# A second Strassen level for one product of each projection, residual sums by accumulating transfers, and longer staging rings, in a four-layer graph-attention kernel

## The chip, the cores and the metric

The kernel runs on one core of a Trainium2 chip. A core has a matrix engine (TensorE, PE in the profile; its weight loads are shown apart as PEld), three engines for elementwise work (VectorE or DVE, ScalarE or ACT, GpSimd or POOL), a queue engine (SyncE or SP) that issues transfers, and 16 DMA engines. Matrix products read on-chip memory (SBUF) and write a small accumulator memory (PSUM, eight banks of 128 x 512 float32); in this kernel DVE and ACT read PSUM, POOL works on SBUF alone. The metric is the device time of one execution in microseconds; less is better.

## What is computed

Input `x` holds 128 graphs of 64 nodes with 512 features, all float32. Four layers follow, each `x = x + f(relu(layernorm(x)))`, and all four see the same 64 x 64 adjacency mask:

```python
# layer 0: 8 heads of 64; q, k, v with bias
x = x + softmax(q @ k.T / 8 + mask) @ v
# layer 1: the same with an output projection
x = x + (softmax(q @ k.T / 8 + mask) @ v) @ Wo + bo
# layer 2: no softmax; one head
rel = adj.T * (q @ k.T);  rel = rel / norm(rel, axis=2)
x = x + rel @ v
# layer 3: attention as in layer 1, then o = o @ Wp + bp
x = x + o + layernorm(o) * gamma + beta
```

## The kernel before

**Tiling.** The 8192 rows are cut into 16 blocks of 512 rows a layer, 64 blocks in all, numbered `n`; `l = n // 16` is the layer. For each block the kernel computes `hT`, the normalised block turned so that features lie on partitions, by a layer norm (DVE statistics, ACT scaling) and transposing transfers (`turn`: a DVE copy that splits each float32 in two 16-bit planes `z`, a DMA transpose into `hp`, an ACT copy back). The four tiles `z` and three tiles `hp` are the "plane rings".

**Projections.** Each weight product of a block is 512 x 512 x 512. `projection` does it by Strassen's method in Winograd's form: seven products of 256 x 256 x 256 in place of eight. The operands are quarters of `hT` and four sums of them in `S` (`sums_x`, on POOL; for the output projection, quarters of `oT` and `SO`), and quarters of the weight and sums of them (`sums_w`). One product is four matmul calls of 128 x 128 stationary by 256 moving columns (`prod_T`, `prod_N`), and each float32 call is two records in the trace. The products run in `ORDER = (1, 6, 5, 2, 7, 3, 4)`; the results are combined by ACT (`s1`, `z5`, `Y11`), DVE (`u2`, `u3`, `Y12`, `Y21`) and POOL (`Y22`). Product 4 is the right lower quarter of the block times the weight sum `WT4`; its result gives the quarter `Y21` with one sum. There are 3, 4, 2 and 4 projections a block in layers 0 to 3. In layer 2, q and k are folded into one matrix beforehand.

**Attention.** `attend` issues the 64 x 64 score products of a block into `so` tiles (two PSUM banks each, two of them), masks them (DVE), subtracts the maximum (POOL), exponentiates (ACT), normalises (POOL), turns the weights by transposing transfers, and issues the products with `v`. `relate` is its counterpart in layer 2. The `mm` tiles (four banks) serve the projections.

**Residuals.** `load_xo` reads the block of `x` again into `xo` and adds a row (bias or beta) to it with four POOL additions. In layer 1 the output projection's `emit_out1` adds straight into `xo`. In layer 3 the projection goes to a tile `o` in the buffer `kT`; `tail3` takes its statistics, adds `o` to `xo` with four POOL additions, then two DVE operations a quarter (`z<-kT,mv,row` and `xo<-z,rs,xo`) finish the block.

**Order.** The program records all operations first (`Plan.record`). `Plan.order` then sorts them: it simulates five queues with a duration for every operation (`duration`), takes on each queue the ready step with the lowest rank, and the order that results is what is issued. On the chip each engine works through its own list in order and waits on semaphores, so a list that was built on a wrong duration makes an engine wait. All recorded operations are issued at line 193. Generators (`spawn`, with delays in "ticks" of one product) decide when a step is recorded.

Of the kernel before, what the change touches and what calls it, by code (L numbers as in the profile page):

```python
# [18 lines left out]
P = 128  # L19
# [24 lines left out]
ORDER = (1, 6, 5, 2, 7, 3, 4)  # L44
ORDER0 = (1, 2, 5, 6, 3, 7, 4)
# [10 lines left out]
class Plan:  # L56
# [4 lines left out]
    def __init__(self, nc):  # L61
        self.nc = nc
        self.steps, self.products = [], []
        self.wrote, self.readers, self.known = {}, {}, {}
        self.group = None
        for e in ("tensor", "vector", "scalar", "gpsimd", "sync"):
            setattr(self, e, Engine(self, e))
# [48 lines left out]
    def add(self, eng, calls, reads, writes, busy, late):  # L116
# [12 lines left out]
        self.steps.append((eng, calls, deps, busy, late))  # L129

    def order(self):
        n = len(self.steps)
        wait = [len(s[2]) for s in self.steps]
        users = [[] for _ in range(n)]
        for i, s in enumerate(self.steps):
            for d in s[2]:
                users[d].append(i)

        rank = [i - RUSH * any(v.tensor.name.startswith("mm_") for c in s[1] for v in c[1][1:] if isinstance(v, bass.AP)) for i, s in enumerate(self.steps)]
# [10 lines left out]
        while len(out) < n:  # L150
# [17 lines left out]
            eng, _, _, busy, late = self.steps[i]  # L168
            if e == "sync":
                moved = max(moved, at + 1400) + late / 180  # L170
                late = moved + 600 - at - busy
            elif e == "vector" and late == PORT:
                busy += max(0.0, free["gpsimd"] - at)
                port = at + busy
            elif e == "gpsimd":
                busy += max(0.0, port - at)
            free[e] = at + busy
            out.append((at, i))
            for u in users[i]:
                same = self.steps[u][0] == e  # L180
                ready[u] = max(ready[u], at + busy + (0.0 if same and e != "sync" else late))
# [36 lines left out]

PORT = 150.5
RUSH = 60  # L220
# [4 lines left out]
def duration(eng, op, aps, a, k):  # L225
# [3 lines left out]
    if eng == "tensor":  # L229
# [3 lines left out]
        pass_ = max(n, P if m > HD else HD) * 0.842  # L233
# [17 lines left out]
    if eng == "gpsimd":  # L251
        if n <= HD:
            return (1010 if ALU.pow in a else 310), 120
        return n * (1.82 if n > D else 2.41), 120
    size = (2 if out.dtype == U16 else 4) * n * out.partition_size()
    return 1270 if k.get("transpose") else 520, size
# [3 lines left out]
def gnn_stack_kernel(  # L260
# [17 lines left out]
    def pool(name, bufs, **kw):  # L278
        return Ring(ctx.enter_context(tc.tile_pool(name=name, bufs=1, **kw)), bufs)

    const, wp, p1, p2, p4, p8, p3 = (
        pool("const", 1), pool("w", 4), pool("p1", 1), pool("p2", 2), pool("p4", 4), pool("p8", 8), pool("p3", 3),
    )
    rows = pool("rows", 3)
    sm = pool("sm", 4)
    dram = ctx.enter_context(tc.tile_pool(name="dram", bufs=1, space=bass.MemoryType.DRAM))
    ps_mm = pool("ps_mm", 4, space=bass.MemoryType.PSUM)
    ps_so = pool("ps_so", 2, space=bass.MemoryType.PSUM)
# [10 lines left out]
    pw = ps_mm.tile([P, KC, P], F32, tag="mm", name="pw")  # L299
# [3 lines left out]
    def dma(dst, src):  # L303
        plan.sync.dma_start(dst, src)

# [36 lines left out]
    def load_w(name, src):  # L342

        w = wp.tile([P, 7, 2, H2], F32, tag="w", name=name)


        def part(i, j):
            return src[i * H2 : (i + 1) * H2, j * H2 : (j + 1) * H2].rearrange("(c p) f -> p c f", p=P)

        dma(w[:, W11], part(0, 0))  # L350
        dma(w[:, W21], part(1, 0))
        dma(w[:, WT3], part(0, 1))
        dma(w[:, W22], part(1, 1))
        return w

    def sums_w(w, eng):
        tt = eng.tensor_tensor
        tt(w[:, WT1], w[:, WT3], w[:, W11], ALU.subtract)
        tt(w[:, WT2], w[:, W22], w[:, WT1], ALU.subtract)
        yield 1  # L360
# [3 lines left out]
    W = {}  # L364

    def weight(name, src, eng=gps):
        W[name] = load_w(name, src)
        yield 4
        yield from sums_w(W[name], eng)

# [4 lines left out]
    first = [load_w("q0", wq0)]  # L375
# [4 lines left out]
    first += [load_w("k0", wk0)]  # L380
# [16 lines left out]
    def raw(tag, src, nm):  # L397
        t = p1.tile([P, KC, D], F32, tag=tag, name=nm)
        for c in range(KC):
            dma(t[:, c, :], src[c * P : (c + 1) * P, :])  # L400
            yield 3
        return t

    def fold():
# [4 lines left out]
        for dc in range(KC):  # L409
            pa = ps_mm.tile([P, D], F32, tag="mm", name=f"pfa_{dc}")  # L410
# [4 lines left out]
            f = p4.tile([P, D], F32, tag="z", name=f"fa_{dc}")  # L415
            act.copy(f, pa)
            yield 1
# [4 lines left out]
        for ec in range(KC):  # L422
            f = p4.tile([P, KC, P], F32, tag="z", name=f"ft_{ec}")
            turn(f, rv[:, ec, :], f"v2_{ec}")
            yield 1
            dma(v2d.rearrange("(c p) e -> p c e", p=P)[:, :, ts(ec, P)], f)
            yield 1
# [17 lines left out]
    hTs, Ss, vs = {}, {}, {}  # L445
    ready = set()

    def turn(dst, src, nm):


        zp = p4.tile([P, D], F32, tag="z", name=f"zp_{nm}").bitcast(U16).rearrange("p (w f) -> p w f", w=2)
        dve.tensor_copy(zp, src.bitcast(U16).rearrange("p (f w) -> p w f", w=2))
        hp = p3.tile([P, 2, KC, P], U16, tag="hp", name=f"hp_{nm}")
# [5 lines left out]
    def layer_norm(n):  # L459
# [19 lines left out]
        if n == 0:  # L479
            for t in range(NT):  # L480
                z = xins[n][t]
                act.activation(z, z, AF.Relu, bias=nb[:, t : t + 1], scale=rs[:, t : t + 1])
                pt = ps_mm.tile([P, KC, P], F32, tag="mm", name=f"pz_{n}_{t}")
# [4 lines left out]
                if t == 1:  # L488
                    for i in range(WARM // 2):
                        pe.transpose(pw[:, i % KC, :], xins[n][0][:, ts(i % KC, P)], ident)  # L490
                (dve.tensor_copy if t else act.copy)(hT[:, :, ts(t, P)], pt)
        for t in range(NT) if n else ():
# [8 lines left out]
    def sums_x(tag, src, nm, eng):  # L501
# [7 lines left out]
        return {1: x11, 2: x12, 3: S[:, 3], 4: x22, 5: S[:, 0], 6: S[:, 1], 7: S[:, 2]}  # L509
# [19 lines left out]

    def projection(prod, w, xop, nm, emit, order=ORDER):  # L530

# [3 lines left out]
        def bank(i):  # L535
            banks[i] = ps_mm.tile([P, D], F32, tag="mm", name=f"pp{i}_{nm}")
# [6 lines left out]
        X = {1: 1, 2: 1, 6: 6, 7: 6, 5: 5, 3: 5, 4: 4}  # L543
        for i in order:
# [4 lines left out]
            prod(ps, w[:, BLOCKS[i]], xop()[i], first)  # L549
# [16 lines left out]
            elif i == 3:  # L566
                emit("Y12", ps, tmp["u2"])
            if i != order[-1]:
# [4 lines left out]
    def emit_plain(region):  # L573

        def emit(what, a, b=None):
# [15 lines left out]
    def emit_bias(region, bias):  # L591

        def emit(what, a, b=None):
# [37 lines left out]
    def scores(qT, kT, g, nm):  # L631

        pss = ps_so.tile([P, 2, 2, KC, G], F32, tag="so", name=f"pss_{nm}")
        for p in range(2):
            for c in range(KC):
                for h, x in QUARTERS:
                    b = h ^ x
                    at = ts(4 * g + 2 * p + b, G)  # L640
                    pe.matmul(
                        pss[half(x), b, p, c, :], qT[half(h), c, at], kT[half(h), c, at], start=True, stop=True
                    )
        return pss

    def attend(n, qT, kT, v, done):

        l = n // NB
        plan.begin()
        psss = [scores(qT, kT, g, f"{n}_{g}") for g in range(2)]  # L650
        plan.end(300)
        ss = [p4.tile([P, 2 * KC, 2, G], F32, tag="s", name=f"s_{n}_{g}") for g in range(2)]
        yield 1
        for s, pss in zip(ss, psss):
            for b in range(2):
                dve.tensor_tensor(
                    s[:, :, b, :], pss[:, b].rearrange("p q c j -> p (q c) j"),
                    MASKS[l].unsqueeze(1).to_broadcast([P, 2 * KC, G]), ALU.add,
                )
            sf = s.rearrange("p q b j -> p (q b) j")  # L660
# [3 lines left out]
            yield 2  # L664
        yield 1
        for s in ss:
# [6 lines left out]
            yield 2  # L673
        yield 1

        aTs = []
        for s in ss:
            aT = s.rearrange("p (q c) b j -> p q c (b j)", q=2)
            aTs.append(aT)
            for p in range(2):  # L680
                if n < N - 1:
                    turn(aT[:, p], s[:, p * KC : (p + 1) * KC].rearrange("p c b j -> p (c b j)"), f"a_{n}_{p}")
                else:
                    pt = ps_mm.tile([P, KC, P], F32, tag="mm", name=f"pa_{n}_{p}")
# [4 lines left out]
                    act.copy(aT[:, p], pt)  # L689
                yield 1  # L690
        yield 1
        yield from done(aTs, v)
# [25 lines left out]
    def load_xo(n):  # L718
# [5 lines left out]
        if l in xo_row:  # L724
            row = R[xo_row[l]]
            for t in range(NT):
                gps.tensor_tensor(xos[n][:, t, :], xos[n][:, t, :], row, ALU.add)
                if t < NT - 1:
                    yield 1
        ready.add(("xo", n))  # L730

    def finish0(n):
        def done(aTs, v):


            assert ("xo", n) in ready and ("v", n) in ready
            plan.begin()
            pos = []
            for g, aT in enumerate(aTs):
                po = ps_so.tile([P, 2, 2, H2], F32, tag="so", name=f"po_{n}_{g}")  # L740
                pos.append(po)
                for p in range(2):
                    for c2 in range(2):
                        for h in range(2):
                            for b, y in QUARTERS:
                                j = b ^ y
                                f = c2 * P + h * HD
                                pe.matmul(
                                    po[half(y), j, p, f : f + HD], aT[half(b), p, 2 * j + c2, half(h ^ b)],
                                    v[half(b), 2 * g + p, j * H2 + f : j * H2 + f + HD], start=True, stop=True,  # L750
                                )
            plan.end(300)
            yield 1
            for g, po in enumerate(pos):
                for j in range(2):
                    xv = xos[n][:, 2 * g : 2 * g + 2, j * H2 : (j + 1) * H2]
                    dve.tensor_tensor(xv, po[:, j], xv, ALU.add)
            yield 1
            store(n, xos[n])
        return done  # L760
# [3 lines left out]
    def finish13(n):  # L764
        def done(aTs, v):

            assert ("v", n) in ready
            oTs[n] = p1.tile([P, KC, T], F32, tag="oT", name=f"oT_{n}")
            plan.begin()
            pos = []  # L770
            for g, aT in enumerate(aTs):
                po = ps_so.tile([P, 2, 2, KC, G], F32, tag="so", name=f"po_{n}_{g}")
                pos.append(po)
                for p in range(2):
                    for c in range(KC):
                        for b, h in QUARTERS:
                            f = c * P + h * HD
                            pe.matmul(
# [346 lines left out]
```

## Time and profile before

| | |
|---|---|
| median of 3 runs | 2844.27 us (2843.87 to 2844.59) |
| the profiled execution's own time | 2844.57 us |
| its span in the profile | 2842.8 us, granted clock 0.999 |
| layer 0, stretch 12 to 660 us: PE / DVE / ACT / POOL busy | 647.9 / 498.5 / 332.2 / 398.5 us |
| layer 2, stretch 1505 to 1985 us | 480.0 / 262.2 / 192.3 / 206.1 us |

The profile page has the busy time of each engine, the span in 40 slices, the DMA queues, the chain of work that ended last, the costliest groups of instructions (tile written, tiles read, count, busy time, mean, and the idle time before them) and the DMA issues. Groups name tiles by kind: `mm<-S,w` is a projection product with moving operand `S` and stationary operand `w`. A mean of one matmul record includes its drain, which overlaps the next; the distance from start to start is its cost.

### The profile page before, as it was taken

What the parts mean: (1) busy time and instruction counts of PE and PEld (TensorE: products, weight loads), DVE (VectorE), ACT (ScalarE), POOL (GpSimd) and SP (SyncE); (2) the same over time, 40 slices, a digit from 0 to 9 for tenths busy, and PEclk for the clock granted to TensorE, in tenths of its full rate; (3) what the DMA queues carried; (4) which work ended last, traced back from release to release, by engine and by line L of the source; (5) the groups of instructions that cost most, each with busy time, mean ns of one, the idle gap of its engine ahead of it and who ended that gap; (6) DMA issues with size and microseconds to landing.
All of it is one profiled execution on the core that took longest, in us unless ns stands there. A gap on an engine that the chain in (4) does not pass through costs nothing.

```text
span 2842.8 us, 62036 instructions
## 1 busy us (share of the span) xinstructions
PE 2828.4 (99%) x25833; PEld 2471.6 (87%) x25833; DVE 2037.6 (72%) x3104; ACT 1248.0 (44%) x1589; POOL 1840.5 (65%) x1349
## 2 busy tenths in 40 slices
PE   9999999999999999999999999999999999999998
PEld 8878888888888888888888888888888888888887
DVE  7767778876767767667666555555688888778787
ACT  4555555454443534534434343443444444444442
POOL 6555566656766667667677334344678687787796
PEclk9999999999999999999999999999999999999999
DMA  6766666556453533533546565756433433433432
GB/s 158 163 137 156 143 146 134 127 128 163 105 120 80 124 95 82 131 85 86 136 114 156 136 162 143 164 128 157 120 86 94 119 86 95 112 91 96 109 84 66
DMA packets 634890, 342.29 MB, mean 120 GB/s; under 512 B 485232, under 2 KB 566384, under 8 KB 634608
## 3 DMA queue, kind: packets, MB, share of 16 engines
q1 hardware_dynamic: 634608, 338.32, 50.0%
q8 instruction: 202, 3.31, 0.5%
q14 instruction: 80, 0.66, 0.1%
HBM read 152.61 MB, written 69.21 MB: 78 GB/s over the span
## 4 chain that ended last, share of the span: by engine, by line
PE 96%; DVE 3%; issue 0%; POOL 0%; DMA 0%; ACT 0%; POOLq 0%; SPq 0%; DVEq 0%
PE mm L193 88%; PE so L193 8%; DVE z L193 1%; DVE st L193 0%; POOL s L193 0%; DVE u L193 0%; DVE sr L193 0%; DVE kT L193 0%; DMA xin<-in_x_dram 0%; DVE mv L193 0%; DVE w L193 0%; DVE xo L193 0%; ACT xin L193 0%; ACT oT L193 0%; POOLq L1120 0%
## 5 line engine op out<-in xcount | busy, mean ns | idle before, releaser
L193 PE MATMUL mm<-S,w 128*128 128x256 f32 x3584 | 817.2, 380 | 0.0
L193 PEld LDWEIGHTS mm<-S,w 128*128 128x128 f32 x3584 | 679.3, 190 | 93.8 <-issue 1.0
L193 PE MATMUL mm<-hT,w 128*128 128x256 f32 x2688 | 629.9, 380 | 4.0 <-DVE kT L193 3.7
L193 DVE TENSOR_TENSOR u<-mm,s 128x512 f32<-128x512 f32 x414 | 284.9, 688 | 480.1 <-PE mm L193 342.3
L193 PEld LDWEIGHTS mm<-hT,w 128*128 128x128 f32 x2688 | 509.6, 190 | 75.5 <-DVE kT L193 5.3
L193 PE MATMUL mm<-w,S 128*128 128x256 f32 x2048 | 472.8, 381 | 0.0
L193 PEld LDWEIGHTS mm<-w,S 128*128 128x128 f32 x2048 | 385.5, 190 | 53.8 <-issue 0.5
L193 ACT COPY hT<-hp 128x1024 uint16<-128x1024 uint16 x252 | 332.7, 1350 | 90.3 <-DMA hp<-z 90.2
L193 PE MATMUL mm<-w,hT 128*128 128x256 f32 x1536 | 366.4, 381 | 0.0
L193 ACT COPY s<-hp 128x1024 uint16<-128x1024 uint16 x188 | 252.3, 1352 | 204.3 <-DMA hp<-z 197.1
L193 ACT COPY s<-mm 128x512 f32<-128x512 f32 x211 | 123.0, 583 | 490.0 <-PE mm L193 419.0
L193 POOL TENSOR_TENSOR s<-s,mx 128x1024 f32<-128x1024 f32 x96 | 183.3, 1911 | 226.9 <-DVE mx L193 224.9
L193 PEld LDWEIGHTS mm<-w,hT 128*128 128x128 f32 x1536 | 289.2, 190 | 40.2 <-DVE v L193 0.2
L193 POOL TENSOR_TENSOR xo<-xo,row 128x512 f32<-128x512 f32 x192 | 286.1, 1510 | 8.4 <-DMA xo<-in_x_dram 5.7
L193 DVE COPY z<-s 128x1024 uint16<-128x1024 uint16 x188 | 278.2, 1501 | 6.7 <-POOL s L193 6.6
L193 DVE COPY z<-xin 128x1024 uint16<-128x1024 uint16 x252 | 245.3, 988 | 37.6 <-ACT xin L193 34.0
L193 ACT ACTIVATE xin<-xin,nb,rs 128x512 f32<-128x512 f32 x256 | 195.4, 808 | 90.5 <-DVE nb L193 89.9
L193 PE MATMUL mm<-w,SO 128*128 128x256 f32 x992 | 224.3, 379 | 0.0
L193 POOL TENSOR_TENSOR qT<-u,z 128x512 f32<-128x512 f32 x64 | 87.5, 1367 | 202.2 <-DVE u L193 189.8
L193 PEld LDWEIGHTS mm<-w,SO 128*128 128x128 f32 x992 | 188.5, 190 | 25.6
L193 POOL TENSOR_TENSOR s<-s,sr 128x1024 f32<-128x1024 f32 x96 | 187.3, 1963 | 34.2 <-DVE sr L193 32.1
L193 ACT ACTIVATE s<-s 128x1024 f32<-128x1024 f32 (+1 forms) x112 | 108.1, 966 | 200.3 <-POOL s L193 144.3
(98 smaller groups left out, 3667.7 us busy)
## 6 DMA issues: line engine op xcount, KB each, us to landing
xin<-x SPq DMA_DIRECT2D x192, 256.0 KB, 4.0
xo<-x SPq DMA_DIRECT2D x64, 512.0 KB, 4.5
xin<-in_x_dram SPq DMA_DIRECT2D x64, 256.0 KB, 3.2
x<-xo SPq DMA_DIRECT2D x64, 256.0 KB, 2.5
x<-xo SPq DMA_DIRECT2D x128, 128.0 KB, 2.5
x<-xo SPq DMA_DIRECT2D x32, 512.0 KB, 3.0
out_dram<-xo SPq DMA_DIRECT2D x30, 512.0 KB, 3.0
xo<-in_x_dram SPq DMA_DIRECT2D x32, 256.0 KB, 3.2
```

The lines of the kernel that those rows point to most:

```text
L193: getattr(getattr(self.nc, eng), op)(*a, **k)
```

## The change

Three things are changed, and some work is moved.

1. In all projections of layers 1 to 3 (`LEVEL2`), product 4 is itself done by Strassen's method: seven products of 128 x 128 x 128 instead of eight parts. They are issued in two groups, "4a" (four calls, after product 5) and "4b" (three, last): `FINER`. New sums of 128 columns are needed of the block (`sums_x`, `needs2`), of the weight (`sums_w`) and of the result (`q`, `close_2`). 159 projections use it; the last block's output projection doesn't, as before.
2. In layers 1 and 3 the row is added to `xo`, and the output projection to `xo`, by accumulating transfers that POOL issues (`add`), one each a block. `emit_out1` goes: layer 1's output projection now goes to `o` in the buffer `kT`, as layer 3's did.
3. The rings of `z` and `hp` grow from 4 to 6 and from 3 to 5. The `s` ring shrinks from 4 to 2. The eight PSUM banks become one pool, taken and given back by name.

Moved: the score products are recorded straight after the k projection, the products with `v` after the next block's q (or before layer 2's v) projection. `Plan.join` makes such a pair of groups one uninterrupted stretch on PE, with a rank ahead of everything.

```diff
 ORDER = (1, 6, 5, 2, 7, 3, 4)
+FINER = (1, 6, 5, "4a", 2, 7, 3, "4b")
+LEVEL2 = {c + l for l in "13" for c in "qkvo"} | {"a2", "v2"}
-RUSH = 60
+RUSH = 100
-        pass_ = max(n, P if m > HD else HD) * 0.842
+        pass_ = max(n * 0.842, 111 if m > HD else HD * 0.842)
+    if "accum_op" in k:
+        return 1100, 2000 + size / 150
...
+    zs, hps = pool("zs", 6), pool("hps", 5)
-    ps_mm = pool("ps_mm", 4, space=bass.MemoryType.PSUM)
-    ps_so = pool("ps_so", 2, space=bass.MemoryType.PSUM)
+    mm = Pool([mm.tile([P, D], F32, tag=f"mm_{i}", name=f"mm_{i}") for i in range(8)])
...
+    def add(dst, src):
+        gps.dma_start(dst, src, accum_op=ALU.add)
...
+        a, b, c, d = [x22[:, j, ts(i, P)] for i in range(2) for j in range(2)]
+        F = fine or [x21[:, j, ts(i, P)] for i in range(2) for j in range(2)]
+        if needs2:
+            tt(F[0], c, d, ALU.add)
+            tt(F[1], F[0], a, ALU.subtract)
+            tt(F[2], a, c, ALU.subtract)
+            tt(F[3], b, F[1], ALU.subtract)
...
+    def prod_2(prod, ps, name, xop, todo):
+        w = W[name][:, WT4]
+        e = W2[name]
+        ws = {1: w[:, 0, :P], 2: w[:, 1, :P], 3: w[:, 1, P:], 4: e[:, 2], 5: e[:, 0], 6: e[:, 1], 7: w[:, 0, P:]}
+        at = {1: (0, 0), 2: (0, 0), 5: (0, 1), 3: (0, 1), 6: (1, 1), 7: (1, 1), 4: (1, 0)}
+        for i in todo:
+            x, out = xop["quarters"][i], quarter(ps, prod, *at[i])
+            a, b = (ws[i], x) if prod is prod_T else (x, ws[i])
+            pe.matmul(out, a, b, start=i == 1, stop=True, skip_group_check=True)
+
+    def close_2(prod, ps, q, base, dst, bias):
+        u2, u3, z5 = q[:, 1], q[:, 2], q[:, 3]
+        y12 = quarter(base, prod, 0, 1)
+        gps.tensor_tensor(y12, y12, u2, ALU.add)
+        y2 = base[:, :, P:] if prod is prod_T else base[:, 1, :].rearrange("p (v f) -> p v f", v=2)
+        gps.tensor_tensor(y2, y2, u3.unsqueeze(1).to_broadcast([P, 2, P]), ALU.add)
+        gps.tensor_tensor(dst[:, 1, P:], base[:, 1, P:], z5, ALU.add)
+        for at in ((slice(None), 0, slice(None)), (slice(None), 1, slice(0, P))):
+            if bias is None:
+                dve.tensor_tensor(dst[at], ps[at], base[at], ALU.add)
+            else:
+                dve.scalar_tensor_tensor(dst[at], ps[at], bias[at[1]], base[at], ALU.add, ALU.add)
...
+            elif i == "4a":
+                q = p1.tile([P, 4, P], F32, tag="q", name=f"q_{nm}")
+                act.copy(q[:, 0], quarter(pv, prod, 0, 0))
+                dst, base, bias = emit("close")
+                if bias is None:
+                    act.copy(q[:, 3], quarter(pv, prod, 0, 1))
+                else:
+                    act.activation(q[:, 3], quarter(pv, prod, 0, 1), AF.Identity, bias=bias[1])
+                dve.tensor_tensor(q[:, 1], quarter(pv, prod, 1, 1), q[:, 0], ALU.add)
+            elif i == "4b":
+                dve.tensor_tensor(q[:, 2], quarter(pv, prod, 1, 1), q[:, 0], ALU.add)
...
+                close_2(prod, pv, q, base, dst, bias)
...
     def load_xo(n):
-            for t in range(NT):
-                gps.tensor_tensor(xos[n][:, t, :], xos[n][:, t, :], row, ALU.add)
+            if l == 0:
...
+            else:
+                add(xos[n], row.unsqueeze(1).to_broadcast([P, NT, D]))
+                yield 3
...
-    def tail1(n):
-        yield 2
+    def tail1(n, o):
+        yield 1
+        add(xos[n], o)
+        yield 4
         store(n, xos[n])
...
     def tail3(n, o):
             stats(mv, t, o[:, t, :], f"o{n}")
-            gps.tensor_tensor(xo[:, t, :], xo[:, t, :], o[:, t, :], ALU.add)
+            if t == NT - 1:
+                add(xo, o)
...
+            values()
             kT = p1.tile([P, KC, T], F32, tag="kT", name=f"kT_{n}")
...
+            begin_scores(n, qT, kT)
-            spawn(attend(n, qT, kT, v, done), 3 if n < N - 1 else 0)
```

## Prediction

> **What bounds the kernel now.** I read the page's totals first, then the chain that ended last, then the PE's waits, its groups by shape, and last the start times on PE.
>
> ```profile
> PE 2828.4 (99%) x25833; PEld 2471.6 (87%) x25833; DVE 2037.6 (72%) x3104; ACT 1248.0 (44%) x1589; POOL 1840.5 (65%) x1349
> ...
> q1 hardware_dynamic: 634608, 338.32, 50.0%
> ...
> PE 96%; DVE 3%; issue 0%; POOL 0%; DMA 0%; ACT 0%; POOLq 0%; SPq 0%; DVEq 0%
> ```
>
> PE is busy 99% of the span and carries 96% of the chain. A busy PE can still be a badly filled one, so the waits of PE and its start times decide:
>
> ```profile
> PE mm L193 <- DVE kT L193: 3.7, 4, 0.9
> PE mm L193 <- POOL ident masks.py:199: 1.3, 1, 1.3
> ```
>
> ```profile
> 2809.24 1.89 PE L193 MATMUL mm<-w,hT 128*128 128x256 f32 x8
> 2810.97 0.60 PE L193 MATMUL mm<-ident,s 128*128 128x128 f32 x4
> 2811.41 1.89 PE L193 MATMUL mm<-w,S 128*128 128x256 f32 x8
> ```
>
> In 2842.8 us PE waited 3.7 us for the `kT` operations of layer 3 and 1.3 us at the start. In the timeline (start, duration, group), a product of 8 records takes 2810.97 - 2809.24 = 1.73 us to the next start: 0.216 us a record of 256 columns, without a gap. So a microsecond taken from PE is one off the end, as long as the other engines keep up. The same lines price the new shape: four 128 x 128 transposes, each with its own weight load, take 2811.41 - 2810.97 = 0.44 us, 0.110 us a record.
>
> ```profile
> L193 PEld LDWEIGHTS mm<-ident,s x16: 139/140/144, 2810.8 to 2816.3; 128*128 128x128 f32 x16
> L193 PE MATMUL mm<-ident,s x16: 272/273/329, 2811.0 to 2816.4; 128*128 128x128 f32 x16
> ```
>
> These loads last 140 ns each, yet come every 110 ns: they overlap.
>
> For the other engines, layers 1 and 3 by stretches (length, then PE, PEld, DVE, ACT, POOL busy, clock, DMA share):
>
> ```profile
> 660.00:1505.00 845.00, 844.39 (x7915) 740.77 (x7914) 585.13 (x848) 363.72 (x471) 573.85 (x412) 1.00 0.44 107
> ...
> 1985.00:2842.00 857.00, 845.90 (x7723) 740.01 (x7721) 685.78 (x963) 354.31 (x437) 655.24 (x473) 1.00 0.39 96
> ```
>
> Layer 3 is the tightest: DVE 80%, POOL 76% of its stretch. Last, an addition that goes (the groups) and landings that price what comes (the DMA issues):
>
> ```profile
> L193 POOL TENSOR_TENSOR xo<-xo,row 128x512 f32<-128x512 f32 x192 | 286.1, 1510 | 8.4 <-DMA xo<-in_x_dram 5.7
> ```
>
> ```profile
> xo<-x SPq DMA_DIRECT2D x64, 512.0 KB, 4.5
> ...
> xo<-x SPq DMA_DIRECT2D x32, 256.0 KB, 3.8
> ```
>
> [...]
>
> **Part 1, the second level.** On PE each of 159 projections loses 4 calls of 256 columns and gains 7 of 128; a call is two records. Removed: 159 x 8 x 0.2156 = 274.2 us. Added: 159 x 14 x 0.110 = 244.9 us. Net -29.4 us. From both sides: at half the 256-column price (0.108) it is -33.8; at 0.140, if each load had to end before the next began, +37.4; break-even is 0.123. I take 0.110, the measured row with the same load.
>
> The switches between 64- and 128-wide products number the same in both instruction lists (227 runs), so they cost nothing new.
>
> What it adds beside PE, a projection: on DVE two sums of 128 columns and the result in 256 + 128, instead of one of 512. From PSUM 512 columns take 685 ns and 256 take 425 (`s<-mm,adj`), so 128 about 295: 3 x 295 + 425 - 685 = +0.62 us. On ACT two copies of 128, 415 ns each from 584 (512) and 471 (256). On POOL two operations of 128 and one of 256. Price of POOL: the uncontended 512-column sum is 1265 ns in the timeline[...]. (Pure proportion gives 316 for 128.) The new sums of `hT` and `oT` are four of 128 each, 1.8 us, for 79 blocks' operands.
>
> **Part 2, the residuals.** POOL loses 128 row additions x 1.51 = 193 us, 60 of `o` x 1.48 = 89 us, and in layer 1 78 us of its projection's sums (64 x 1.57 less the 16 x 1.41 that take their place). It gains 63 issues. Sum over the kernel: 159 x 1.64 + 79 x 1.8 - 360 = +43 us[...]: about 1950 us, 69% of the span. In layer 3: 655 - 97 - 89 + 64 x 1.64 + 31 x 1.8 + 34 = 664 us, 79% instead of 76%. DVE in layer 3: 686 + 64 x 0.62 = 725 us of some 845, 86%. In layer 1, DVE 585 + 24 = 609 of 835 and POOL about 580. No engine takes PE's place on average; DVE in layer 3 has some 7 us a block left.
>
> The wait that is added: in layer 3 the first `xo<-z,rs,xo` on DVE waits for the accumulate of `o`. Two accumulates stand side by side in POOL's list there, the row into one `xo` and `o` into the other, 1 MB each. The landing rows (256 KB in 3.8 us, 512 KB in 4.5) give 0.7 us more per 256 KB, so 5.9 us for 1 MB; if accumulating moves the bytes twice, 8.7, and the second of a pair lands some 13 us after its issue; at best, a plain copy alone, 6. By PE's order, `o` is complete some 2.5 us after its last product, and DVE reaches the waiting operation about 14 us after that product: 10 us of cover behind the issue. Queued behind it on DVE is `q` of the k projection, for which 4b of that projection waits 4 us later, and then the scores. So up to about 14 us after issue it costs PE little. I take 13 and a cost of 0 to 1 us in a few blocks. In layer 1 the only readers behind are the store and the next writing of `kT`, some 18 us away: nothing.
>
> **Part 3, rings and order.** DVE's copies into `z` waited for the ring 3.1 us in all (`DMA hp<-z`), off the chain: nothing to gain. Attention has to keep its time: counted on PE with the prices above, from scores to products with `v` the list of before leaves 29.6 us in layer 1 and 33.1 in layer 3, the new one 30.8 and 32.5. From the last k product to the scores it was 5.2 and 8.6 to 10.3 us, and is 6.9 and 5.2; in layer 0 it falls from 7 to 14 us to 1.7. What must fit there in layer 0 are two DVE operations of 478 ns behind the PE's drain (380 - 216 ns), some 1.2 us: it fits if DVE is free. In layer 3 it is 0.3 (DVE) + 0.73 (POOL) + 0.72 (DVE) = 1.8 us, with 3.4 to spare for queues. I put 3 us on all new short stops together, as much as the layer-3 stops of before (3.7 us) that the new order may lose.
>
> **Sum.** Against the profiled span 2842.8: -29.4 + 3 = 2816.4; the runs' median 2844.27 lies 1.5 us above the span, so 2818.
>
> **Rivals.**
> - A, the forecast: PE stays full, 2818; own range 2807 (0.108 a record, stops of before gone) to 2826.
> - B, half the gain: the new small operations on POOL and the short distances behind k make PE stop about 0.4 us at each of some 30 blocks of layers 1 and 3, 12 us: 2830. For it: DVE at 86%, the planner's price of 308 ns for a POOL operation that I put at 455. Against: the list of before, made by the same rules, left 5 us of waits.
> - C, slower: the accumulate is late. Beyond 14 us after issue, each further us stops PE for as much in the 15 blocks of layer 3 that have the DVE wait. It eats the gain from 16 us on; at 20 us it costs 15 x 6 = 90 us, 2905. For it: the pair shares 16 DMA engines with the transposes (3.3 us each in the page)[...]. Against: the landing rows of before.
> - D, weight loads bind at 140 ns: 2844 + 37 = 2882. Against: 110 ns in the trace.
>
> **How the numbers follow.** A 0.54, B 0.24, C 0.16, D 0.06. The range 2807 to 2842 holds A but for its lower edge, all of B and the mildest of C. A run of this kernel can be told from another at about 0.2%, 5.7 us: faster means under 2838.6. A and nearly all of B are faster, 0.77; the rest of B and a mild C are within, 0.06; C and D are slower, 0.17.
>
> **What would show it.** Right: 14 records of 128 columns in 1.54 us; PE's busy time near 2800 us, its waits under 10 us; in layer 3 POOL near 660 and DVE near 725 us. B: PE waits for `kT`, `q` or `u` in most blocks. C: DVE `xo` waiting for a DMA in layer 3, landings over 14 us. D: 128-column records 140 ns apart. The forecast is wrong if PE's waits grow by more than 10 us, wherever from.

## The result, and the profile after

The changed kernel takes 2920.45 us (median of 4 runs, 2918.91 to 2922.63) against 2844.43 us for the kernel before (2843.87 to 2845.23): 1.0268 times as long, 95% interval 1.025 to 1.0285. The forecast was 2818 us, a gain, so its sign was wrong.

The page of the changed kernel (its span is 2919.6 us, its lines are numbered anew, the recorded operations are now at L215):

```profile
PE 2833.1 (97%) x26787; PEld 2500.6 (86%) x26787; DVE 1966.7 (67%) x3533; ACT 1318.9 (45%) x1923; POOL 2020.8 (69%) x2009
...
q1 hardware_dynamic: 634608, 338.32, 49.0%
q0 software_dynamic: 21360, 66.06, 12.6%
...
PE 86%; DMA 7%; POOL 2%; ACT 1%; DVE 1%; issue 1%; SPq 0%; POOLq 0%; ACTq 0%; DVEq 0%
...
xo<-row POOLq DMA_DIRECT2D x32, 1024.0 KB, 8.3
xo<-kT POOLq DMA_DIRECT2D x30, 1024.0 KB, 13.6
```

PE was busy 99% and is busy 97%. Idle time of PE went from 2842.8 - 2828.4 = 14.4 us to 2919.6 - 2833.1 = 86.5 us: 72.1 us of the 76.8 us by which the span grew. The other 4.7 us are longer busy time, where 29 fewer had been expected. The chain of work that ended last had 0% of transfers before and now has 7%. The queue q0 is new: 63 accumulating transfers of 1 MB (1024 KB). The last two lines are DMA issues, with the median time to landing in us: the row alone lands after 8.3 us, `o` (here `kT`), the second of a pair, after 13.6.

What PE waited for (total us, times, longest):

```profile
PE mm L215 <- ACT s L215: 59.9, 16, 7.0
PE mm L215 <- ACT z L215: 7.4, 3, 4.9
```

The `s` is `s1`, ACT's copy of product 1. By the kernel, product 2 is summed onto product 1 in the same PSUM bank, so PE can't start it before ACT has made this copy. Before the change PE waited for it once, 0.2 us. By stretches (columns as in the prediction: length, then PE, PEld, DVE, ACT, POOL busy, clock, DMA share, GB/s), at the times that were layers 1 and 3 in the kernel before:

```profile
660.00:1505.00 845.00, 787.12 (x7438) 695.39 (x7437) 514.19 (x898) 364.77 (x561) 575.41 (x603) 0.97 0.61 131
...
1985.00:2842.00 857.00, 851.91 (x8096) 759.65 (x8095) 637.03 (x1163) 388.93 (x575) 694.67 (x707) 1.00 0.63 138
```

Layer 1 now ends some 83 us later, so the second row begins inside layer 2; from 2080 us to the end, which is layer 3, PE is busy 98%. So layer 3, where the prediction had looked for trouble, is nearly full. Layer 1 isn't: 58 us are missing in the first row, and the mean clock falls to 0.97. No engine is near its limit in it (DVE 61%, POOL 68%).

The first score record of each of the 48 blocks with scores of layers 0, 1 and 3 marks a block's start in the trace. The times between such starts, in us:

| from the start of scores to the start of scores | before | after | difference |
|---|---|---|---|
| start of the span to the last block of layer 0 | 667.8 | 662.1 | -5.7 |
| last of layer 0 to last of layer 1 | 818.0 | 906.7 | **+88.7** |
| last of layer 1 to first of layer 3 (all of layer 2) | 524.7 | 520.2 | -4.5 |
| first to last of layer 3 | 781.1 | 777.6 | -3.5 |
| from there to the end | 51.2 | 53.0 | +1.8 |

Of the +88.7, 6.1 are in the first three blocks of layer 1. The 13 that follow took 52.8 us each before and take 57.9 to 66.3 now, one stop in each. One of them shows the cause. In the timeline (start, duration, what), first POOL's and SP's transfers, then ACT, then PE:

```profile
1243.05 1.37 POOL L215 DMA_DIRECT2D xo<-row  x1
1243.91 1.44 POOL L215 DMA_DIRECT2D xo<-kT  x1
...
1236.29 24.23 SPq L215 DMA_TRANSPOSE hp<-z  x7
...
1248.20 1.51 ACT L215 ACTIVATE xin<-xin,nb,rs 128x512 f32<-128x512 f32 x2
1259.43 3.73 ACT L215 COPY hT<-hp 128x1024 uint16<-128x1024 uint16 x3 [9.73 <-DMA hp<-z]
1263.03 0.57 ACT L215 COPY s<-mm 128x512 f32<-128x512 f32 x1
...
1258.79 1.05 PE L215 MATMUL mm<-hT,w 128*128 128x128 f32 x8
1263.65 2.98 PE L215 MATMUL mm<-hT,w 128*128 128x256 f32 x8 [3.81 <-ACT s L215]
1266.43 4.36 PE L215 MATMUL mm<-S,w 128*128 128x256 f32 x16
1270.62 0.83 PE L215 MATMUL mm<-hT,w 128*128 128x128 f32 x6
```

POOL issues both accumulating transfers within 0.9 us, 2 MB. Just then SP issues the transposes for the `hT` of the next block. ACT's list has the copies of those transposes first and `s1` of the projection behind them, so it idles 9.73 us in front of a transpose, and `s1` waits though its data are there. PE comes to product 2 at 1259.7 and stands for 4.0 us. The chain of waits in this stretch (start, duration, what) says the same:

```profile
1205.76 39.50 PE mm L215 x311
1245.25 14.16 DMA hp<-z
...
1259.43 1.76 ACT hT L215 x2
...
1263.03 0.58 ACT s L215
...
1263.65 11.47 PE mm L215 x47
```

A transpose that landed 14.16 us after its issue is on it. The instructions on `hp` from 1000 to 1500 us, issue to landing:

```profile
DMA to landing us min/median/max: 3.0/3.3/14.7
```

The median is that of before (3.3), the worst was 6.5 before. The stop has a second cost, seen in the clock (third column from the right) of short windows:

```profile
1260.00:1264.00 4.00, 0.35 (x2) 0.32 (x3) 0.37 (x1) 4.00 (x5) 3.08 (x6) 1.00 1.11 326
1264.00:1268.00 4.00, 4.00 (x12) 3.24 (x11) 0.62 (x2) 2.80 (x7) 3.00 (x3) 0.57 1.03 298
1268.00:1272.00 4.00, 4.00 (x23) 3.59 (x23) 1.76 (x4) 0.00 (x0) 3.92 (x7) 1.00 0.73 275
```

After the stop PE is busy again, at 0.57 of its clock for 4 us: the trace has the granted clock at 0.50 for 3.4 us, from 1264.5. Each of the thirteen stops (3.8 to 7.0 us) is followed by such a stretch, as is one of 4.95 us from 2109.3; the five of 1.2 to 1.9 us (from 727.3, 1570.0, 1588.8, 1647.0 and 2892.1) are not. In `e1_pool_sums_l1` below, a stop of 2.44 us (from 1552.9) is followed by 3.4 us at 0.50 too. From start to start the 8 records at 1263.65 take 2.78 us in place of 1.73, the 16 after them 4.19 in place of 3.45: 1.8 us. With the stop of 4.0 this is 5.8 us, and the block is 58.1 - 52.1 = 6.0 us longer than a block of the same code without a stop. Of the thirteen stops ten are followed by 3.4 us at half clock and three by 6.8 us: 27 us lost, most of the 30 us by which PE's busy time missed its fall.

### The profile page after: what moved, and what is told of

It is laid out like the page before. It is cut to its first block, busy times and chain, and to the rows that moved or that the text cites. A ratio compares the mean times of both kernels' runs of the same rounds, so it can differ in the third digit from the quotient of the medians.

```text
span 2919.6 us, 65816 instructions
## 1 busy us (share of the span) xinstructions
PE 2833.1 (97%) x26787; PEld 2500.6 (86%) x26787; DVE 1966.7 (67%) x3533; ACT 1318.9 (45%) x1923; POOL 2020.8 (69%) x2009
## 4 chain that ended last, share of the span: by engine, by line
PE 86%; DMA 7%; POOL 2%; ACT 1%; DVE 1%; issue 1%; SPq 0%; POOLq 0%; ACTq 0%; DVEq 0%
PE mm L215 86%; DMA hp<-z 6%; ACT hT L215 1%; POOL S L215 1%; POOL s L215 1%; DMA xo<-w 0%; POOL w L215 0%; ACT s L215 0%; DVE xo L215 0%; DVE st L215 0%; DVE z L215 0%; POOL SO L215 0%; POOL u L215 0%; DMA xin<-in_x_dram 0%; DMA w<-a2d 0%
## 5 line engine op out<-in xcount | busy, mean ns | idle before, releaser
L215 PE MATMUL mm<-S,w 128*128 128x256 f32 x3584 | 822.0, 382 | 7.4 <-ACT z L215 7.4
L215 PEld LDWEIGHTS mm<-S,w 128*128 128x128 f32 x3584 | 686.5, 192 | 105.3 <-ACT z L215 8.9
L215 PE MATMUL mm<-hT,w 128*128 128x256 f32 (+1 forms) x3040 | 633.5, 354 | 60.2 <-ACT s L215 58.7
L215 PEld LDWEIGHTS mm<-hT,w 128*128 128x128 f32 x3040 | 518.7, 194 | 124.2 <-ACT s L215 61.8
L215 DVE TENSOR_TENSOR u<-mm,s 128x512 f32<-128x512 f32 x414 | 284.0, 686 | 414.1 <-PE mm L215 257.9
L215 PE MATMUL mm<-w,S 128*128 128x256 f32 x2048 | 469.8, 381 | 0.0
L215 PEld LDWEIGHTS mm<-w,S 128*128 128x128 f32 x2048 | 384.8, 190 | 53.3 <-issue 0.7
L215 ACT COPY hT<-hp 128x1024 uint16<-128x1024 uint16 x252 | 329.6, 1345 | 192.9 <-DMA hp<-z 192.7
L215 POOL TENSOR_TENSOR s<-s,mx 128x1024 f32<-128x1024 f32 x96 | 181.6, 1916 | 297.2 <-DVE mx L215 294.5
L215 PE MATMUL mm<-w,hT 128*128 128x256 f32 (+1 forms) x1696 | 349.8, 348 | 1.3 <-ACT s L215 1.3
L215 PEld LDWEIGHTS mm<-w,hT 128*128 128x128 f32 x1696 | 285.4, 191 | 33.3 <-ACT s L215 1.7
L215 ACT COPY s<-hp 128x1024 uint16<-128x1024 uint16 x188 | 250.0, 1349 | 116.7 <-DMA hp<-z 111.8
L215 ACT COPY s<-mm 128x512 f32<-128x512 f32 x211 | 122.6, 582 | 354.8 <-PE mm L215 239.1
L215 DVE COPY z<-s 128x1024 uint16<-128x1024 uint16 x188 | 212.4, 1151 | 66.3 <-POOL s L215 66.2
L215 DVE COPY z<-xin 128x1024 uint16<-128x1024 uint16 x252 | 227.2, 923 | 40.3 <-ACT xin L215 39.8
L215 POOL TENSOR_TENSOR qT<-u,z 128x512 f32<-128x512 f32 x64 | 95.2, 1487 | 202.3 <-DVE u L215 192.8
L215 POOL TENSOR_TENSOR u<-u,q 128x128 f32<-128x128 f32 (+1 forms) x288 | 201.4, 710 | 36.7 <-DVE q L215 27.2
L215 ACT ACTIVATE xin<-xin,nb,rs 128x512 f32<-128x512 f32 x256 | 196.4, 809 | 64.7 <-DVE nb L215 61.3
L215 PE MATMUL mm<-w,SO 128*128 128x256 f32 x992 | 224.5, 379 | 0.0
L215 PEld LDWEIGHTS mm<-w,SO 128*128 128x128 f32 x992 | 188.4, 190 | 25.6
L215 POOL TENSOR_TENSOR S<-hT 128x512 f32<-128x512 f32 x126 | 162.6, 1291 | 49.7 <-ACT hT L215 49.7
L215 POOL TENSOR_TENSOR s<-s,sr 128x1024 f32<-128x1024 f32 x96 | 185.9, 1944 | 12.2 <-DVE sr L215 9.5
## 6 DMA issues: line engine op xcount, KB each, us to landing
xo<-kT POOLq DMA_DIRECT2D x30, 1024.0 KB, 13.6
```

The source lines that it names most:

```text
L215: getattr(getattr(self.nc, eng), op)(*a, **k)
```

## Experiments

The theory (T): in layer 1, row and `o` are a pair of accumulating transfers that fill the 16 DMA engines (share 1.07 from 1251 to 1260 us) while the transposes of the next block's `hT` are due; ACT waits for those in order with `s1` behind. Rivals: (R1) the second level itself is too much for POOL, ACT or the order; (R2) POOL's issues and its access to SBUF are at fault, not the DMA engines; (R3) a list that was built on wrong durations, which would be cured by telling the planner. The block times below are between starts as in the table.

**Layer 1's sums back on POOL** (`e1_pool_sums_l1`)

```diff
-            if l == 0:
+            if l in (0, 1):
                 for t in range(NT):
                     gps.tensor_tensor(xos[n][:, t, :], xos[n][:, t, :], row, ALU.add)
...
-        add(xos[n], o)
+        for t in range(NT):
+            gps.tensor_tensor(xos[n][:, t, :], xos[n][:, t, :], o[:, t, :], ALU.add)
```

> Layer 1 alone goes back to residual sums by POOL (four row additions and four additions of o a block); everything else as changed. Theory T (the two accumulating transfers of a block hold the DMA engines, the transposes of the next block's hT crawl beside them, ACT waits for them with k's copy s1 queued behind, PE stops): the stops of 4 to 7 us on ACT s go, a block of layer 1 takes 52 to 53 us instead of 58, the granted clock returns to 0.998 or more, time 2830 to 2845. Rival R (the small operations of the second level make POOL and ACT late): POOL has still more to do, the stops stay, time 2900 or more.

2833.94 us (2833.33 to 2835.47), 0.9965 of before [0.9952, 0.9978]. Layer 1's blocks take 52.1 us. The timeline of ACT at the same place, the waits of PE, and the landings of `hp` in the same window:

```profile
1251.56 1.41 ACT L215 COPY hT<-hp 128x1024 uint16<-128x1024 uint16 x1
1255.59 0.58 ACT L215 COPY s<-mm 128x512 f32<-128x512 f32 x1 [2.63 <-issue]
1256.80 1.36 ACT L215 COPY hT<-hp 128x1024 uint16<-128x1024 uint16 x1 [0.63 <-DMA hp<-z]
```

```profile
PE mm L215 <- ACT z L215: 4.0, 2, 2.2
```

```profile
DMA to landing us min/median/max: 3.0/3.1/5.4
```

The wait for `s` is gone from the head of PE's waits (0.9 us are left), and transposes land within 5.4 us. `s` is now copied at 1255.59 with no transpose waited for ahead of it. So 86.5 us come back with layer 1's transfers, and R1 falls: the second level is still there in every projection. T, R2 and R3 are left, since this edit changes POOL's and ACT's lists too.

**Only the row back on POOL** (`e2_pool_row_l1`: the first hunk of e1 alone)

> In layer 1 only the row is added by POOL again; o is still added by one accumulating transfer. T: the queue in front of the transposes is half as long (5 us instead of 11), ACT's waits of some 10 us shrink to under 5, the stops of PE go or fall under 1 us; time 2830 to 2865. R: 2900 or more. If a single transfer beside the transposes is already enough to stop PE, 2880 to 2900.

2851.10 us (2848.39 to 2855.44), 1.0025 [1.0017, 1.0032]. One transfer a block, `o`, stays. The wait for `s` goes; PE now waits 16.0 us, 12 times, for DVE's `kT`, and blocks take 52.9 to 57.5 us from the sixth on. Beside `o` alone the transposes land within 5.5 us in the window of before, and ACT waits 2.9 us for one at most, not 10.3. What makes these blocks longer than those of e1, which has the same four row additions, was not traced.

**The same two transfers, apart** (`e5_row_later_l1`: the row's transfer waits for the next block's v projection)

```diff
-        yield 4
+        yield 14 if l == 1 and k < NB - 1 else 4
...
                 add(xos[n], row.unsqueeze(1).to_broadcast([P, NT, D]))
+                if l == 1 and k < NB - 1:
+                    plan.steps[-1][2].add(plan.products[-1])
```

> In layer 1 the accumulating transfer of the row is issued in the v projection of the next block, away from that of o and from the transposes of hT; number of operations unchanged. T: as with the row on POOL, 2830 to 2865. R, and any account by the number of operations: no difference, 2910 to 2930.

2836.59 us (2834.29 to 2840.47), 0.9974 [0.9964, 0.9984]. The page's DMA issues, and `hp` in the window of before:

```profile
xo<-row POOLq DMA_DIRECT2D x32, 1024.0 KB, 8.4
xo<-kT POOLq DMA_DIRECT2D x30, 1024.0 KB, 8.1
```

```profile
DMA to landing us min/median/max: 3.0/4.3/5.2
```

Same transfers, same bytes, the same number of issues by POOL; `o` now lands after 8.1 us, transposes within 5.2, blocks take 52.1 us. ACT's list is the same as in the changed kernel too: over two steady blocks its 76 operations stand in the same order, `s1` behind the same copies. This separates T from R2: neither the transfers nor POOL's work in issuing them cost the 80 us, but where the row's transfer stands.

The packet records say in part how a transpose is held up. While `o` is moved (1250 to 1256 us in the changed kernel) its packets of 8 KB and the 256-byte packets of the transposes come in nearly equal numbers: 20 and 22, 30 and 31, 20 and 20, 30 and 29 in successive microseconds from 1251. When the transfer is over, up to 1086 of the small ones are served in one. An 8 KB packet takes 638 ns, a small one beside it 32 ns (18 when alone). If 16 engines did one of each in turn, that would be 16 / 0.670 = 24 of each a microsecond, an estimate beside the 20 to 31 seen; a transpose has 1024. So the packets of the two queues come nearly one for one here, 8 KB against 256 bytes. It isn't the whole delay. The first small packet came over 4 us after the issue at 1245.25, and in the 3 us after the last large one only 238 to 493 small ones started a microsecond. Why is open.

**One level, with transfers** (`e3_one_level`)

```diff
-LEVEL2 = {c + l for l in "13" for c in "qkvo"} | {"a2", "v2"}
+LEVEL2 = set()
```

> The second level is off everywhere (product 4 in one piece), the accumulating transfers, the rings and the order of the change stay. T: the collision is still there, 13 stops a run in layer 1, time 2900 to 2955 (2920 plus up to 29 for PE's work, less what the emptier POOL gives back). R: the stops go, 2840 to 2850.

3059.71 us (3048.01 to 3069.06), 1.0756 [1.0728, 1.0784], more than either expectation. The second level is not the cause: without it, the transfers cost more. Blocks take some 62 us in layer 1 and some 58 in layer 3. PE's waits, then the timeline at one stop in layer 3 (POOL, SP, ACT):

```profile
PE mm L215 <- ACT s L215: 96.7, 32, 10.2
PE mm L215 <- ACT z L215: 56.0, 12, 7.0
```

```profile
2619.01 1.66 POOL L215 DMA_DIRECT2D xo<-row  x1
...
2619.64 27.18 SPq L215 DMA_TRANSPOSE hp<-z  x5
...
2625.83 1.36 ACT L215 COPY s<-hp 128x1024 uint16<-128x1024 uint16 x1 [6.85 <-DMA hp<-z]
```

It is a like stop in another layer: the order has moved, and now layer 3's transfers too fall beside transposes. A pair isn't needed for it: the row's transfer stands alone here, `o` follows at 2630.41. I had not expected that the place would move with the number of products.

**No transfers at all** (`e6_no_transfers`: e1, the row on POOL in every layer, and `tail3` adding `o` on POOL; `e7_one_level_no_transfers`: the same with `LEVEL2 = set()`)

```diff
-            if l == 0:
+            if True:
...
-            if t == NT - 1:
-                add(xo, o)
+            gps.tensor_tensor(xo[:, t, :], xo[:, t, :], o[:, t, :], ALU.add)
```

> No accumulating transfer anywhere: rows and o are added by POOL in layer 3 as well; second level, rings and order as changed. T: layer 1 as with POOL's sums there alone, 52 us a block. In layer 3 POOL gets some 186 us more on the 684 it is busy in 845, over its share if it also has to keep time: 2835 to 2880. If POOL copes, 2830.

> Neither the second level nor any accumulating transfer; what is left of the change is the rings, the PSUM pool and the order of scores and values. T: no stops, 52.8 us a block in layers 1 and 3, 2838 to 2852; so the transfers alone are what costs over 200 us in the kernel with one level and with them. If order or rings were at fault there, 2900 or more.

e6: 2899.70 us (2896.57 to 2900.68), 1.0193 [1.0178, 1.0208], above what I expected. e7: 2839.21 us (2838.75 to 2840.71), 0.9983 [0.9976, 0.999]. Layer 3's stretch in e6:

```profile
1985.00:2842.00 857.00, 814.36 (x7641) 720.23 (x7634) 675.39 (x1086) 368.03 (x540) 794.82 (x754) 0.98 0.38 93
```

POOL is busy 93% of it and blocks take 50 to 65 us; layer 1 is at 52.1 as in e1. In this order layer 3 can't have the second level and its residual sums on POOL together. PE's waits in e7:

```profile
PE mm L215 <- POOL ident masks.py:199: 1.3, 1, 1.3
PE mm L215 <- ACT xin L215: 1.1, 2, 0.8
```

With the new order alone, one level and no transfers, PE has no stop worth naming. The two parts of the change by two choices each, in us:

| | no transfers | transfers in layers 1 and 3 | transfers in layer 3 only |
|---|---|---|---|
| one level | 2839.2 (e7) | 3059.7 (e3) | |
| two levels | 2899.7 (e6) | 2920.5 (the change) | 2833.9 (e1) |

The parts don't add: each effect has its sign from where it meets the other.

**The planner told of the transfers** (`e8_planner_knows`: one accumulating transfer after the other, on the same engines as SP's; `e9_pool_l1_planner_knows`: with e1 as well)

```diff
             if e == "gpsimd":
                 busy += max(0.0, port - at)
+                if moves:
+                    moved = max(moved, at + 2000) + 6200
+                    late = moved + 600 - at - busy
```

> The changed kernel, all operations kept; only the planner is told that an accumulating transfer of 1 MB holds the DMA engines for 6.2 us, so that it lands later itself and the transposes behind it land later too (before, it had the transfer beside an otherwise free DMA). Theory T: the lists then put ACT's waits for transposes and PE's products where the chip has them; most stops of layer 1 go without a single operation less, 2830 to 2860. If the collision costs whatever the order, since the transposes themselves are too late for S and the k projection, 2890 to 2920.

> Layer 1's sums on POOL, and the planner counts 6.2 us of DMA for each accumulating transfer of layer 3. T: little is left to mend in layer 3 (52.1 us a block there already), so 2825 to 2838. If the planner's new times move transposes and copies in layer 3 for the worse, 2845 or more.

e8: 2870.62 us (2866.79 to 2877.01), 1.0095 [1.008, 1.011], between the two expectations. After one block of 79.8 us layer 1's blocks take 52.1 to 53.2 (the last 47.8), but layer 3's become uneven (48.3 to 65.1). A steady block of layer 1 (POOL, SP, ACT; lines are numbered anew), and the landings of `hp` from 1000 to 1500 us:

```profile
1161.40 1.37 POOL L218 DMA_DIRECT2D xo<-row  x1
1162.26 1.41 POOL L218 DMA_DIRECT2D xo<-kT  x1
...
1166.11 13.05 SPq L218 DMA_TRANSPOSE hp<-z  x4
...
1173.92 0.58 ACT L218 COPY s<-mm 128x512 f32<-128x512 f32 x1 [5.73 <-PE mm L218]
...
1178.12 1.35 ACT L218 COPY hT<-hp 128x1024 uint16<-128x1024 uint16 x1
```

```profile
DMA to landing us min/median/max: 3.0/3.3/12.2
```

The pair stands where it stood, 0.9 us apart and just ahead of the transposes; `o` still lands after 13.5 us and a transpose after up to 12.2. Yet from 1150 to 1500 us PE shows no wait: ACT's list now has `s1` in front of the copies of the late transposes. So the crowding alone costs these blocks nothing. (PE has the same projection products in the same order through this stretch; a few operations of DVE and POOL have moved too.) e5 kept ACT's list and took the crowding away, e8 kept the crowding and changed ACT's list; either gives blocks of 52.1 us, so the stop needs both. R3 is thus half of the cause: the planner gave each transfer a landing of its own and nothing to the transposes beside it, and so put `s1` behind copies that would be late. A better account removes two thirds of the loss, 49.8 of 76.0 us; the one long block and layer 3's uneven ones, which keep the rest, I did not trace. e9: 2839.19 us (2835.05 to 2849.72), 0.999 [0.998, 1.0001]: better than the planner's edit alone, worse than e1 alone.

**The rings** (`e10_pool_l1_short_rings`: e1 with the rings at their old lengths)

```diff
-    zs, hps = pool("zs", 6), pool("hps", 5)
+    zs, hps = pool("zs", 4), pool("hps", 3)
```

> Layer 1's sums on POOL, the rings of z and hp back to 4 and 3. If the rings do nothing, as forecast, within 3 us of 2834. If the longer rings are what lets transposes run ahead of a transfer, PE stops more and it is 2840 or more; if they only bunch the transposes, 2830 or less.

2915.81 us (2913.72 to 2916.78), 1.025 [1.0237, 1.0263], 82 us more than e1. Layer 1 keeps its 52.1 us; two of every four blocks of layer 3 take 62 to 67. The timeline at one of them (POOL, SP, ACT, PE):

```profile
2412.27 1.41 POOL L215 DMA_DIRECT2D xo<-row  x1
...
2401.64 23.25 SPq L215 DMA_TRANSPOSE hp<-z  x5
...
2426.51 1.33 ACT L215 COPY s<-hp 128x1024 uint16<-128x1024 uint16 x1 [8.87 <-DMA hp<-z]
...
2430.80 5.49 PE L215 MATMUL mm<-hT,w 128*128 128x256 f32 x16 [7.66 <-ACT qT L215]
```

In the changed kernel layer 3's pair (at 2533.34 and 2534.21, for one) lies where no transpose is issued, between 2530 and 2553 us. With short rings SP issues transposes right across the row's transfer (`o` follows at 2429.66), ACT waits 8.87 us for one of them, and PE waits for the copy `qT` that stands behind it in ACT's list. In this order the longer rings are what keeps transfers and transposes apart.

**Towards a better version** (`e11_pool_l1_and_last`: e1, and the last residual but one on POOL in `tail3`; `e12_level2_in_2_and_3`: e1 without the second level in layer 1)

```diff
-            if t == NT - 1:
+            if n == N - 2:
+                gps.tensor_tensor(xo[:, t, :], xo[:, t, :], o[:, t, :], ALU.add)
+            elif t == NT - 1:
                 add(xo, o)
```

```diff
-LEVEL2 = {c + l for l in "13" for c in "qkvo"} | {"a2", "v2"}
+LEVEL2 = {c + "3" for c in "qkvo"} | {"a2", "v2"}
```

> Layer 1's sums on POOL, and o of the last block but one is added by four POOL operations instead of a transfer. In the last stretch the chain runs through that transfer (13.5 us) and then DVE. T: the end comes 3 to 6 us earlier, 2828 to 2831. If the end hangs on something else, 2834 as before.

> Layer 1 with one level and with POOL's sums; second level in layers 2 and 3 only, layer 3 with transfers. With the second level layer 1 gains 0.66 us a block when it runs steadily but stops in its first blocks. If those stops come from the second level's operations there, they go: 2828 to 2833. If they come from something else (weights, the turn from layer 0), layer 1 loses its 8 to 10 us of gain: 2840 to 2845.

e11: 2835.31 us (2833.89 to 2837.34), 0.9968 [0.9956, 0.998], no gain over e1: the transfer at the end is replaced by POOL additions on the chain. e12: 2833.45 us (2833.31 to 2835.19), 0.9963 [0.995, 0.9977], the same as e1. In its layer 1 a block takes 52.8 in place of 52.1 us, but the first three together take 134.2 in place of 147.3. The second level gains nothing in layer 1 as a whole. e1 and e12 beat both kernels, by about 0.35% over the one before.

## Why the prediction was wrong

- **PE's saving** was right in mechanism. 128-column records come every 0.1117 us (6 in 1271.29 - 1270.62 = 0.67 us of the changed kernel), where I had 0.110 from the transposes: 274.2 - 2226 x 0.1117 = 25.6 us saved, not 29.4. A steady block of four projections went from 52.8 to 52.1 us, and 4 x (8 x 0.2156 - 14 x 0.1117) = 0.64. Rival D, 140 ns a record, is out. The switches between 64- and 128-wide products show in the trace of before: a product of 8 records beside one takes 1.82 to 1.84 us (711.86 to 717.54 us), not 1.73. What the prediction calls the drain is a record's mean length less the distance to the next start (380 and 216 ns there); the profile models the ends, so what PE does in these 164 ns is not shown.
- **The step that failed**: "In layer 1 the only readers behind are the store and the next writing of `kT`, some 18 us away: nothing." I asked who reads what the transfer writes, and not who shares the 16 DMA engines with it for the 13 us that I had given the pair myself, nor what is queued behind them on ACT. The transposes stood in the same window, and `s1` behind them; e5 and e8 show that both were needed. This step was worth 92 us: 13 blocks of layer 1 take 768.9 us and would take 13 x 52.1 = 677.3.
- **Rival C** had the right resource ("the pair shares 16 DMA engines with the transposes") and the wrong place. It made DVE's wait in layer 3 late. That wait came in 13 blocks, 46.2 us in all and 5.2 at most, and PE never stood for it: the cover counted there was enough, and the pair's 13 us were right (13.6), as was 8.7 for one alone (8.1 to 8.3). Both came from the guess that accumulating moves the bytes twice, which no run tests. One sum of C is off: 2818 + 90 is 2908, not 2905.
- **"Nothing to gain" from the rings** was wrong. I counted their waits in the kernel before, where no transfer needed room beside the transposes. Beside e1 they are worth 82 us, 73 of them between the first and last block of layer 3 (e10).
- **"3 us on all new short stops"**: PE's idle time grew by 72, and by 10.8 even in e1. Rival B's places (`kT`, `q`, `u`) were not it either; layer 0's 1.7 us distance fitted, its blocks are steady at 40.7 us but for the first and one of 54.4.
- **POOL's issue**, put at 1.1 us in the 1950 and the 664 as in the change's `duration`, takes 1.39 (median); POOL as a whole 2020.8 us, not 1950. The prediction's 1.64 us a projection and 1.8 us for the four new sums were estimates of mine, and near: a small sum takes 0.46 us for 128 columns and 0.73 for 256 uncontended, so 2 x 0.46 + 0.73 = 1.65 and 4 x 0.46 = 1.84. Layer 3's POOL, 684.3 us in e1's stretch from 1985, is above the 664. None of this decided anything.
- **DVE in layer 3** is 642 us in e1, where layer 3 lies nearly where it lay before, not 725. I added what comes and kept the rest at its old duration, but with the residual sums off POOL some of DVE's large operations are shorter (last section).
- **The test that was set** held: "The forecast is wrong if PE's waits grow by more than 10 us, wherever from."
- Even without the stops the gain isn't 26 us. In e1 PE is busy 2806.9 us, 21.5 less than before, but idle 25.2 us, 10.8 more. Beside e7, which has the new order without second level and transfers, e1 is only 5.3 us faster. Against before, e1 is 5.5 us shorter in layer 3 and 4.8 in layer 2, and 4.5 longer in layer 1, whose first three blocks take 147.3 us in place of 131.7. What fills those three blocks, and whether smaller packets for `o` would let the transposes through, was not tried.

## What to carry to other kernels

When an addition becomes a transfer, its price is not its landing but what else is on the DMA engines from issue to landing: lay that window over the transfers of the other queues, and look at what waits in order behind those. Here either half was a cure for the steady blocks of layer 1. Moving one transfer, with no byte less and ACT's order unchanged, took back 84 us, more than the 76 that were lost; leaving the transfers and putting ACT's copy for PE ahead of the late transposes freed those blocks as well. And where PE stood some 4 us, it lost about half as much again in clock (1.8 us beside 4.0).

## What the hardware showed that I had not expected

- Large and small packets came nearly one for one: beside an accumulating transfer of 8 KB packets (638 ns each) a transpose of 256-byte packets got 20 to 31 a microsecond instead of the 1086 and 1070 of the two microseconds from 1259. An accumulating packet of 2 KB took 189 ns (median), an ordinary one 84.
- DVE's large operations in layer 3 changed with where the residual sums are done; that POOL's work beside them is the reason is not shown. With layer 3's residual sums on transfers, `z<-s` takes 1102 ns and `xo<-z,rs,xo` 912 (means in e1); with those sums on POOL (e6), 1391 and 1107. The kernel before had 1444 and 1077. It isn't a fixed surcharge: `z<-kT,mv,row` goes from 923 (e1) to 1155 ns (e6), but is 791 in e7, which has the sums on POOL too.
